# The last routing of a second expert stage placed in fewer tiles, and one exponential per routing

## The chip, the cores and the metric

The kernel runs on one core of a Trainium2 chip. Its five engines are TensorE (PE, with its weight loads shown as PEld), VectorE (DVE), ScalarE (ACT), GpSimd (POOL) and SyncE (SP); each works through its own queue of instructions in order, and they wait for each other by semaphores. The metric is the device time of one execution in microseconds; the number compared is the median of several executions.

## The reference

The program is a row of blocks on x of 16 x 256 = 4096 tokens with 128 features, all in float32: a mixture of experts, grouped-query attention, the same mixture of experts again, a block of eight "zones", a latent attention, and the zones again. Only the mixture of experts is touched. It is used twice with the same weights, each time as `x = x + 0.5 * ffn(layernorm(x))`:

```python
def _L0_ffn_ref(x, gate_w, experts_gate_up, experts_down, shared_gate_w, shared_up_w, shared_down_w, shared_expert_gate_w):
    logits = x_flat @ gate_w.T                       # 8 experts
    scores = softmax(logits)
    _, topk_ids = top_k(scores, 2)
    w = scores * one_hot(topk_ids).sum(axis=1)
    gu = einsum('nh,eih->nei', x_flat, experts_gate_up)   # 2 x 176
    h = silu(gu[..., :176]) * gu[..., 176:]
    out = einsum('neh,ne->nh', einsum('nei,ehi->neh', h, experts_down), w)
    shared = silu(x_flat @ shared_gate_w.T) * (x_flat @ shared_up_w.T) @ shared_down_w.T
    return out + sigmoid(x_flat @ shared_expert_gate_w.T) * shared
```

So each token has two of eight experts, weighted by their softmax scores, and a shared expert weighted by a sigmoid.

## The kernel before

The 4096 tokens are held in SBUF as eight blocks of 512 (`xs`), and routed in four pairs of blocks, 1024 tokens each (pairs 0 to 3). Each expert has a region of rows in DRAM (`moe_rows`). An expert stage has these parts:

*Routing of a pair* (`route_pieces`, fifteen pieces when it is coarse): four of statistics, a first guess and a refinement of the inverse root (VectorE), two that write the normalised tokens (`pair_xn`, half on ACT and half on VectorE), two that transpose them (TensorE, copies on VectorE and ACT), one for the logits of eight experts and, in a ninth column, of the sigmoid; then `choose` (VectorE: the two best experts), `count_before` (VectorE: prefix sums, and ACT: the exponentials), `place_pair` (three small matmuls, L579 to L585, turn the counts into a row for every token and choice; then sixteen indirect DMAs of POOL, L601, scatter the tokens to these rows) and `weights_of`. In `count_before` ACT computes exp of the logits less their maximum (L562, `moe_ex`) and, in a second instruction, exp of the negated ninth column (L565, `moe_ws`); the sigmoid follows on VectorE by L566 and L567. Exp and Silu are functions of different tables on ACT, and a change of table is an instruction of its own in the trace (ACT_TABLE_LOAD).

*Plans* (`plan_tiles`, three pieces by `table_pieces`): from the counts so far VectorE writes a table of tiles, each a run of 256 rows of one expert. Plans are made after two, three and four pairs. With two pairs 9 tiles are certain, with three 17, and the last plan has the rest of the 39. The last plan also makes SyncE read the eight counts (L658) and send eight stores of zeros (L665) behind the experts' last rows.

*Tiles* (`expert_tiles`): for each of the 39 tiles SyncE reads the table (L852), loads the expert's weights (L860, `moe_we`, six buffers) and the rows (L864, `moe_xg`, six buffers); TensorE transposes the rows (L881, copied to `moe_xT` by VectorE, L883), multiplies up (L893), ACT applies Silu (L895, L896), VectorE multiplies (L899, L902, into `moe_h` and `h`), TensorE multiplies down (L915, L920), ACT copies the result (L928) and sends it to DRAM (L929). Iteration k turns tile k, does up of tile k - 1 and down of tile k - 2, and then calls the pieces that `hooks[k]` names. Rows of tile 17 and later wait for all scatters of all four pairs; earlier ones only for those of the pairs that their plan knew.

After the tiles POOL gathers the results of each token (L956), VectorE adds them, and the remaining blocks of the shared expert (L803 to L832) are computed.

The first expert stage routes all four pairs before its tiles. The second one routes pairs 0, 1 and 2 beside attention (`beside_attention`), with the plans for two and three pairs; the routing of pair 3 and the last plan are hooks of its first tiles in `moe_second`. A tile scheduler puts instructions into the engines' queues by the order of the calls and by modelled times, so pieces of a hook are interleaved with tiles near it and not strictly behind one of them. PSUM tiles of kind `pb` have two buffers, shared by turns, transposes, logits and `place_pair`.

Of the kernel before, what the change touches and what calls it, by code (L numbers as in the profile page):

```python
# [12 lines left out]
F32 = mybir.dt.float32  # L13
I32 = mybir.dt.int32
U32 = mybir.dt.uint32
AF = mybir.ActivationFunctionType
ALU = mybir.AluOpType
# [3 lines left out]
P = 128  # L21
# [9 lines left out]
E0, I0, SI0, K0 = 8, 176, 352, 2  # L31
# [20 lines left out]
def macaron_kernel(ctx: ExitStack, tc: tile.TileContext, a: dict, out: bass.AP):  # L52
# [3 lines left out]
    nc = tc.nc  # L56
# [5 lines left out]
    small = ctx.enter_context(tc.tile_pool(name="small", bufs=3))  # L62
# [309 lines left out]
    NPT = 2 * NTT  # L372
# [46 lines left out]
    def begin_routing(S):  # L419
        shape = [P, NPAIR, K0, NPT]  # L420
        S["mine"] = routed.tile(shape + [E0], F32, name="moe_mine")
        S["at"] = routed.tile(shape, F32, name="moe_at")
        S["w"] = routed.tile(shape, F32, name="moe_w", bufs=2)
        S["index"] = routed.tile(shape, U32, name="moe_index", bufs=2)
        S["count"] = region_of

        S["row"] = region_of
        S["phases"] = []
# [87 lines left out]
    def choose_pieces(S, q):  # L516
        return [partial(choose, S, q), partial(count_before, S, q)]

    def choose(S, q):

        if q == 0:
            begin_routing(S)
        mine = S["mine"][:, q]
        shape = [P, NPT, E0]

        def wide(v):
            return v.unsqueeze(2).to_broadcast(shape)

        first = sooner.unsqueeze(1).to_broadcast(shape)
        lg = S["lg"][q]  # L530
        m = small.tile([P, NPT], F32, name="moe_m")
        nc.vector.tensor_reduce(m, lg[:, :, 0:E0], AX.X, ALU.max)
        less = small.tile(shape, F32, name="moe_less")
        nc.vector.tensor_tensor(less, lg[:, :, 0:E0], wide(m), ALU.subtract)
        key = small.tile(shape, F32, name="moe_key")
        nc.vector.scalar_tensor_tensor(key, less, 0.0, first, ALU.is_equal, ALU.mult)
        top = small.tile([P, NPT], F32, name="moe_top")
        nc.vector.tensor_reduce(top, key, AX.X, ALU.max)
        nc.vector.tensor_tensor(mine[:, 0], key, wide(top), ALU.is_equal)
        others = small.tile(shape, F32, name="moe_others")  # L540
        nc.vector.scalar_tensor_tensor(others, mine[:, 0], -3e38, less, ALU.mult, ALU.add)
        nc.vector.tensor_reduce(top, others, AX.X, ALU.max)
        nc.vector.tensor_tensor(key, others, wide(top), ALU.is_equal)
        nc.vector.tensor_tensor(key, key, first, ALU.mult)
        nc.vector.tensor_reduce(top, key, AX.X, ALU.max)
        nc.vector.tensor_tensor(mine[:, 1], key, wide(top), ALU.is_equal)
        S["less"][q] = less

    def count_before(S, q):

        mine = S["mine"][:, q]
        lg, less = S["lg"][q], S["less"][q]
        shape = [P, NPT, E0]
        s = sums[q % 2]
        now = slice(AHEAD, AHEAD + NPT)
        nc.vector.tensor_tensor(s[:, 0, now], mine[:, 0], mine[:, 1], ALU.add)
        for k in range(3):
            by = slice(AHEAD - 2**k, AHEAD - 2**k + NPT)
            nc.vector.tensor_tensor(s[:, k + 1, now], s[:, k, now], s[:, k, by], ALU.add)

        ex = small.tile(shape, F32, name="moe_ex")
        nc.scalar.activation(ex, less, AF.Exp)  # L562
        S["ex"][q] = ex
        ws = routed.tile([P, NPT], F32, name="moe_ws", bufs=NPAIR)
        nc.scalar.activation(ws, lg[:, :, E0], AF.Exp, scale=-1.0)  # L565
        nc.vector.tensor_scalar(ws, ws, 2.0, 2.0, ALU.mult, ALU.add)  # L566
        nc.vector.reciprocal(ws, ws)  # L567
        S["ws"][q] = ws

# [66 lines left out]
    def table_pieces(S, q):  # L636

        steps = []

        def piece(k):  # L640
            if k == 0:
                steps.append(plan_tiles(S, q))
            next(steps[0], None)

        return [partial(piece, k) for k in range(3)]
# [342 lines left out]
    def all_results(S):  # L988
        for t in range(2):
            fetch_results(S, t)  # L990
        for t in range(NBLK):
            pending[t] = add_results(S, t)

    def route_pieces(S, q, fine=False):
        return (
            pair_pieces(S, q, fine)
            + choose_pieces(S, q)
            + [partial(place_pair, S, q), partial(weights_of, S, q)]
        )
# [30 lines left out]
    def last_shared(S, t, end, after):  # L1030


        for k in range(t, end):
            pieces = shared_pieces(S, k)
            for f in pieces[:-1]:
                f()
            if k == t + 1:
                with tc.issue_after(added["up"].ins):
                    ready = after()
            pieces[-1]()  # L1040
        return ready
# [28 lines left out]
    def moe_second(S, after):  # L1070
        third = route_pieces(S, 3)
        hooks = {
            0: third[0:2],
            1: third[2:4],
            2: third[4:6],
            3: third[6:8],
            4: third[8:10],
            5: third[10:12],
            6: third[12:13],
            8: third[13:15],  # L1080
        }
        for k, f in enumerate(table_pieces(S, 4)):
            hooks[10 + k] = [f]
        for q in range(NPAIR):
            hooks[20 + 4 * q] = [partial(result_rows, S, q)]
        expert_tiles(S, hooks)
        all_results(S)
        return last_shared(S, 3, NBLK, lambda: after()())
# [714 lines left out]
    with in_pools(2, dict(pa=3)):  # L1803
        ready = moe_second(moes[1], partial(zones_pre, 0))
# [121 lines left out]
```

## Time and profile before

| | us |
|---|---|
| median of 4 runs | 1409.63 |
| lowest, highest | 1407.43, 1414.92 |
| the profiled execution | 1411.91 |
| its span | 1410.0 |

The stages by the profile's windows and lines: the first expert stage to about 200 us, attention to about 604 us, the tiles of the second expert stage from 604 to 721 us, its shared expert and results to about 767 us, then zones, latent attention and zones. Busy over the whole span: PE 1324.5 us (94%), DVE 953.0 (68%), ACT 668.1 (47%), POOL 448.8 (32%). The mean clock granted to TensorE is 0.983.

In the profile a line of a group or a timeline starts with its source line and engine; `out<-in` names the tiles written and read; a bracket at the end gives the time that the engine was idle before it and what ended that. SPq, ACTq and POOLq are the queues' own instructions, DMA issues among them.

### The profile page before, as it was taken

The numbers are of one execution on the slowest core, as the hardware profiler recorded it, in microseconds if no ns is written. First come the engines' busy times: TensorE is split into PE (matmuls) and PEld (weight loads), VectorE is DVE, ScalarE is ACT, GpSimd is POOL, SyncE is SP. The second block draws the span as 40 slices with busy tenths as digits, with TensorE's granted clock in tenths as the row PEclk, the third lists the DMA queues.
The fourth block names the chain that finished last, engine by engine and source line by source line (L and its number), as shares of the span: only waits on it lengthen the run. The fifth ranks groups of instructions, "written<-read, shape, count | busy, mean of one in ns | idle before, by whom it ended". The sixth has DMA issues, their size and how long they took to land.

```text
span 1410.0 us, 24848 instructions
## 1 busy us (share of the span) xinstructions
PE 1324.5 (94%) x7939; PEld 897.4 (64%) x7939; DVE 953.0 (68%) x3353; ACT 668.1 (47%) x1492; POOL 448.8 (32%) x515
## 2 busy tenths in 40 slices
PE   6898989999999999888999999999999999999998
PEld 4586754455555553466766878876555655688887
DVE  7755758788988874465757666665887888745341
ACT  4333421455555556343433334336777776634342
POOL 4770047420000404214027600014776765500000
PEclk9999999999999998999999999999999999999999
DMA  5297822100000100168834452520000000253532
GB/s 144 68 262 211 223 77 52 29 23 10 10 10 13 36 2 31 39 169 229 233 86 142 135 185 90 177 93 0 2 1 1 1 1 1 91 186 106 186 119 91
DMA packets 96497, 125.71 MB, mean 89 GB/s; under 512 B 12656, under 2 KB 68848, under 8 KB 96368
## 3 DMA queue, kind: packets, MB, share of 16 engines
q1 hardware_dynamic: 66960, 97.11, 22.5%
q0 software_dynamic: 8192, 16.79, 4.0%
q10 hardware_dynamic: 21216, 10.23, 2.4%
q8 instruction: 64, 1.05, 0.3%
q14 instruction: 65, 0.53, 0.1%
HBM read 98.40 MB, written 22.81 MB: 86 GB/s over the span
## 4 chain that ended last, share of the span: by engine, by line
PE 66%; DVE 19%; ACT 5%; DMA 3%; issue 3%; POOL 2%; SPq 1%; DVEq 0%; POOLq 0%; ACTq 0%
PE pb L1468 11%; PE pa L1454 10%; PE score L1197 6%; PE pb L1286 5%; PE exp L1209 4%; PE pa L893 3%; ACT ex L1640 3%; DVE nm L1633 3%; PE pa L803 3%; DMA moe_xg<-moe_rows 2%; PE score L1623 2%; PE pa L823 2%; PE pb L1582 2%; PE pa L915 1%; DVE pT L1670 1%
## 5 line engine op out<-in xcount | busy, mean ns | idle before, releaser
L1650 POOL TENSOR_SCALAR ex<-ex,rs 128x256 f32<-128x256 f32 x192 | 174.8, 928 | 69.2 <-DVE rs L1648 43.0
L956 POOL DMA_INDIRECT y<-moe_y,moe_index x128 | 124.1, 969 | 222.9 <-issue 194.7
L601 POOL DMA_INDIRECT moe_rows<-pair_xn,moe_slot x128 | 124.3, 971 | 201.0 <-DVE moe_slot L597 62.4
L1454 PE MATMUL pa<-xnT,zone_m 128*128 128x256 f32 x768 | 183.0, 381 | 2.0 <-DMA zone_m<-in_w_z_dram 1.1
L1462 ACT ACTIVATE zh<-pa 128x1024 f32<-128x1024 f32 x96 | 97.7, 1023 | 182.9 <-PE pa L1454 182.8
L1468 PE MATMUL pb<-zh,zone_m 128*128 128x256 f32 x768 | 176.8, 381 | 0.0
L1240 ACT ACTIVATE pT<-exp 128x512 f32<-128x512 f32 x224 | 124.2, 595 | 106.1 <-PE exp L1209 100.3
L1209 PE MATMUL exp<-qT,kT 32*128 32x512 f32 x480 | 168.6, 642 | 0.0
L1236 DVE TENSOR_REDUCE nm<-score 128x2 f32<-128x512 f32 x224 | 143.7, 683 | 33.1 <-PE exp L1209 32.2
L1197 PE MATMUL score<-kT,qT 32*128 32x256 f32 x960 | 163.7, 406 | 1.4 <-DVE nm L1236 1.2
L1468 PEld LDWEIGHTS pb<-zh,zone_m 128*128 128x128 f32 x768 | 144.7, 190 | 19.7 <-issue 0.3
L1454 PEld LDWEIGHTS pa<-xnT,zone_m 128*128 128x128 f32 x768 | 141.4, 190 | 23.3 <-DMA zone_m<-in_w_z_dram 2.4
L1197 PEld LDWEIGHTS score<-kT,qT 32*128 32x128 f32 x960 | 97.3, 184 | 80.9 <-DVE nm L1236 47.8
L1640 ACT ACTIVATE ex<-score,nm 128x256 f32<-128x256 f32 x256 | 117.5, 472 | 33.9 <-DVE nm L1634 22.4
L893 PE MATMUL pa<-moe_xT,moe_we 128*128 128x256 f32 (+1 forms) x468 | 118.3, 385 | 2.8 <-DVE moe_xT L883 2.1
L893 PEld LDWEIGHTS pa<-moe_xT,moe_we 128*128 128x128 f32 (+1 forms) x468 | 79.9, 186 | 15.5 <-DVE moe_xT L883 2.8
L895 ACT ACTIVATE moe_sg<-pa 128x256 f32<-128x256 f32 x78 | 29.9, 383 | 119.6 <-PE pa L893 119.6
L1633 DVE TENSOR_REDUCE nm<-score 128x4 f32<-128x1024 f32 x64 | 77.3, 1207 | 6.9 <-PE score L1623 6.9
L1668 PEld LDWEIGHTS turn<-ident,ex 128*128 128x128 f32 x512 | 57.5, 143 | 38.1 <-POOL ex L1650 21.1
L1623 PE MATMUL score<-kt,qa 64*128 64x256 f32 x512 | 78.0, 417 | 1.5 <-ACT ex L1640 1.5
L1668 PE MATMUL turn<-ident,ex 128*128 128x128 f32 x512 | 71.8, 281 | 5.3 <-ACT pT L1670 3.5
L1286 PE MATMUL pb<-pT,v 128*32 128x512 f32 x512 | 71.4, 626 | 2.8 <-ACT pT L811 1.5
(302 smaller groups left out, 2281.2 us busy)
## 6 DMA issues: line engine op xcount, KB each, us to landing
zone_m<-in_w_z_dram SPq DMA_DIRECT2D x96, 512.0 KB
moe_we<-in_w_ex_dram SPq DMA_DIRECT2D x78, 312.0 KB
moe_xg<-moe_rows SPq DMA_DIRECT2D x78, 128.0 KB
moe_y<-moe_yt ACTq DMA_DIRECT2D x78, 128.0 KB
x<-in_x_dram SPq DMA_DIRECT2D x8, 256.0 KB
moe_rows<-pair_xn,moe_slot POOLq DMA_INDIRECT x128
moe_rows<-zero_rows SPq DMA_DIRECT2D x16, 128.0 KB
y<-moe_y,moe_index POOLq DMA_INDIRECT x128
```

What stands on the lines that cost most here:

```text
L601: nc.gpsimd.indirect_dma_start(out=S["views"].pop()[:, :], out_offset=bass.IndirectOffsetOnAxis(ap=slot[:, k, i : i + 1], axis=0), in_=S[" ...
L893: nc.tensor.matmul(dst, q["w"][:, cols], q["xT"], start=True, stop=True)
L1197: nc.tensor.matmul(sc[:, j % 2, :], qa[rows, j, ts(b * NST + st, P)], kt[rows, ts(b, SEQ)], start=True, stop=True,)
L1209: nc.tensor.matmul(sc, kt[rows, ts(b * NST + s, P)], qa[rows, ts(half, 2), ts(b, SEQ)], start=True, stop=True,)
L1236: reduced["last"] = nc.vector.tensor_reduce(new["nm"][:, s, g1 + c, ts(half, 2)], scores[c], AX.X, ALU.max, negate=True)
L1240: nc.scalar.activation(old["pT", half][:, s, g0 + c, :], exps[c], AF.Exp)
L1286: nc.tensor.matmul(q["po"][ts(g, 32)], v[:, b * NST + s, ts(g, 32)], pT[:, s, g, :], start=(s == 0), stop=(s == NST - 1),)
L1454: nc.tensor.matmul(ps[:, f, :], mats[b * K1 + k][:, 0, ts(f, P)], xnT[:, ts(b, SEQ)], start=True, stop=True,)
L1468: nc.tensor.matmul(pz, mats[b * K1 + k][:, 1, ts(f, P)], h[:, f, :], start=(f == 0), stop=(f == NF1 - 1),)
L1640: nc.scalar.activation(ex[:, k, :], sc[:, k, :], AF.Exp, bias=nm[:, k : k + 1], scale=SCALE1, accum_out=rs[:, k : k + 1],)
L1650: nc.gpsimd.tensor_scalar(ex[:, k, :], ex[:, k, :], rs[:, k : k + 1], None, ALU.mult)
L1668: nc.tensor.transpose(pt[:, k, :], ex[:, k, ts(s, P)], ident)
```

## The change

Two things. In `choose` and `count_before` the negated ninth column is written by VectorE into a ninth column of the tile that already holds the logits less their maximum; one exponential of ACT over nine columns then serves the softmax and the sigmoid. This holds for all eight routings of the two stages. In `moe_second` the pieces of pair 3's routing are called at the hooks of tiles 0 to 4, four to a tile, instead of 0 to 8, two to a tile; `place_pair` stands at hook 3 instead of 6, and the three pieces of the last plan at hooks 8 to 10 instead of 10 to 12.

```diff
@@ choose
-        less = small.tile(shape, F32, name="moe_less")
+
+        both = small.tile([P, NPT, E0 + 1], F32, name="moe_less")
+        less = both[:, :, 0:E0]
         nc.vector.tensor_tensor(less, lg[:, :, 0:E0], wide(m), ALU.subtract)
...
-        S["less"][q] = less
+        nc.vector.tensor_scalar(
+            both[:, :, E0 : E0 + 1], lg[:, :, E0 : E0 + 1], -1.0, None, ALU.mult
+        )
+        S["less"][q] = both
@@ count_before
-        ex = small.tile(shape, F32, name="moe_ex")
-        nc.scalar.activation(ex, less, AF.Exp)
-        S["ex"][q] = ex
+        ex = small.tile([P, NPT, E0 + 1], F32, name="moe_ex")
+        nc.scalar.activation(ex, S["less"][q], AF.Exp)
+        S["ex"][q] = ex[:, :, 0:E0]
         ws = routed.tile([P, NPT], F32, name="moe_ws", bufs=NPAIR)
-        nc.scalar.activation(ws, lg[:, :, E0], AF.Exp, scale=-1.0)
-        nc.vector.tensor_scalar(ws, ws, 2.0, 2.0, ALU.mult, ALU.add)
+        nc.vector.tensor_scalar(ws, ex[:, :, E0], 2.0, 2.0, ALU.mult, ALU.add)
         nc.vector.reciprocal(ws, ws)
@@ moe_second
         hooks = {
-            0: third[0:2],
-            1: third[2:4],
-            2: third[4:6],
-            3: third[6:8],
-            4: third[8:10],
-            5: third[10:12],
-            6: third[12:13],
-            8: third[13:15],
+            0: third[0:4],
+            1: third[4:8],
+            2: third[8:12],
+            3: third[12:13],
+            4: third[13:15],
         }
         for k, f in enumerate(table_pieces(S, 4)):
-            hooks[10 + k] = [f]
+            hooks[8 + k] = [f]
```

More of the change, by code (lines that the diff above doesn't have):

```diff
@@ L546, in choose @@
         nc.vector.tensor_tensor(mine[:, 1], key, wide(top), ALU.is_equal)
-        S["less"][q] = less
+        nc.vector.tensor_scalar(
+            both[:, :, E0 : E0 + 1], lg[:, :, E0 : E0 + 1], -1.0, None, ALU.mult
+        )
+        S["less"][q] = both
     def count_before(S, q):
         mine = S["mine"][:, q]
-        lg, less = S["lg"][q], S["less"][q]
-        shape = [P, NPT, E0]
         s = sums[q % 2]
```

## The prediction, made before the changed kernel was run

> **What bounds the kernel now.** The program is one row of stages, and only two are touched in a way that can move the end: the routing beside the first tiles of the second expert stage (604 to 721 us) and, by one small edit, each of the eight routings. I first cut that stage into three windows (busy us, and count, of PE, PEld, DVE, ACT, POOL; then clock, DMA share, GB/s).
>
> ```profile
> 604.00:634.00 30.00, 26.36 (x165) 20.97 (x164) 22.25 (x86) 16.26 (x34) 1.92 (x2) 1.00 0.69 189
> 634.00:671.00 37.00, 31.28 (x184) 23.54 (x183) 20.80 (x74) 13.57 (x36) 15.36 (x16) 1.00 0.80 224
> 671.00:721.00 50.00, 49.35 (x303) 39.65 (x303) 34.31 (x115) 21.11 (x56) 0.00 (x0) 1.00 0.74 204
> ```
>
> From 671 us on TensorE works 49.35 of 50 us: nothing is to be had there. The 67 us before hold 57.64 us of matmuls, so some 9.4 us of idle time is the most that better timing of routing and plan could give. The list of waits of TensorE between 600 and 730 us (total, times, longest) says what ends that idle time:
>
> ```profile
> PE pb L881 <- DMA moe_xg<-moe_rows: 5.0, 6, 1.8
> PE pa L893 <- DVE moe_xT L883: 2.1, 3, 1.3
> PE pa L915 <- DVE h L902: 1.8, 5, 0.6
> ```
>
> The gathered rows of a tile come late, six times; the rest is VectorE. Next the timeline of TensorE, SyncE's queue and POOL (start, us, what, [idle before, and its releaser]):
>
> ```profile
> 649.49 0.44 PE L881 MATMUL pb<-ident,moe_xg 128*128 128x128 f32 x2 [1.39 <-DMA moe_xg<-moe_rows]
> 659.77 0.44 PE L881 MATMUL pb<-ident,moe_xg 128*128 128x128 f32 x2 [1.81 <-DMA moe_xg<-moe_rows]
> 663.04 0.44 PE L881 MATMUL pb<-ident,moe_xg 128*128 128x128 f32 x2 [0.91 <-DMA moe_xg<-moe_rows]
> 671.13 1.46 PE L893 MATMUL pa<-moe_xT,moe_we 128*128 128x256 f32 x6
> 673.66 1.46 PE L893 MATMUL pa<-moe_xT,moe_we 128*128 128x256 f32 x6
> ```
> ```profile
> 638.66 0.34 SPq L860 DMA_DIRECT2D moe_we<-in_w_ex_dram  x1
> 641.92 4.37 SPq L665 DMA_DIRECT2D moe_rows<-zero_rows  x8
> 646.47 0.40 SPq L864 DMA_DIRECT2D moe_xg<-moe_rows  x1
> 654.13 0.35 SPq L860 DMA_DIRECT2D moe_we<-in_w_ex_dram  x1
> 657.64 0.37 SPq L864 DMA_DIRECT2D moe_xg<-moe_rows  x1
> ```
> ```profile
> 634.60 0.96 POOL L601 DMA_INDIRECT moe_rows<-pair_xn,moe_slot  x1 [28.30 <-DVE moe_pick L625]
> 653.56 0.96 POOL L601 DMA_INDIRECT moe_rows<-pair_xn,moe_slot  x1 [0.30 <-issue]
> ```
>
> I count tiles by the matmul groups of L893, six records a tile: 9 groups start before 634.8 us, 6 more before 653.5 and 5 more before 671.1, so those that start at 626.55, 645.68, 653.57 and 671.13 us are tiles 7, 13, 15 and 20. An undisturbed tile takes 673.66 - 671.13 = 2.53 us. Two things are late. First, SyncE's queue: the weights of tile 14 go out at 638.66, then come the last plan's counts and eight zero stores (641.92 for 4.37 us), and only at 646.47 the rows of tile 14: 7.8 us without a fetch, and TensorE waits 1.39 us for them at 649.49. Second, the sixteen scatters of pair 3 on POOL: 634.60 to 653.56, that is 18.96 / 15 = 1.264 us each; the last lands 3.75 us after its start by the chain of waits, and tile 17, the first that needs it, has its rows asked for only at 657.64, 3.16 us behind its weights (654.13 + 0.35). TensorE waits 1.81 and 0.91 us. From tile 15 to tile 20 it takes 671.13 - 653.57 = 17.56 us instead of 5 x 2.53 = 12.65.
>
> **The change part by part.** *One exp for a routing.* Removed, eight times: one ACT exponential of 128x8 (0.16 us from PSUM, 0.22 from SBUF, rows of L565). Added, eight times: one VectorE multiply of 128x8; the row of L566, same form, takes 0.16 us. The remaining exp is 72 wide instead of 64: 0.256 us, at most 72/64 of that, +0.03. Beside attention (250 to 450 us TensorE is busy 197.08 of 200) I cost this at nothing; without that cover it is 3 x 0.16 = 0.5 us. In the first stage the multiply stands ahead of the first scatter, and the new order of instructions also puts one 128x512 multiply (L812, 0.68 us) ahead of the prefix sums and one normalise (0.26) and one statistic (0.2) behind them: +0.1 + 0.6 - 0.3 - 0.2 = +0.2 us to the first scatter at 24.12. POOL then works through 64 scatters without a gap, so the first tiles and the last plan inherit +0.2. The other pairs have room: slots of pairs 2 and 3 are ready at 48.7 and 65.8 us, POOL reaches them at 24.12 + 32 x 1.266 = 64.6 and 84.9. Bounds: -0.5 (the removed exps all count, 8 x 0.16 less the multiplies) to +0.7 (the L812 in full).
>
> *Table loads.* In the order of instructions four table loads go, because a routing's two exps no longer straddle a Silu. The rows:
>
> ```profile
> 621.36 1.28 ACT L562 ACT_TABLE_LOAD   x1 [0.43 <-ACT moe_yt L928]
> 623.68 1.28 ACT L895 ACT_TABLE_LOAD   x1
> 626.15 1.28 ACT L565 ACT_TABLE_LOAD   x1
> 627.64 1.28 ACT L895 ACT_TABLE_LOAD   x1
> ```
>
> One pair goes here (626.15, 627.64), one at 576.36 and 582.03. At 582.03 the load stands before a Silu whose input is ready near 582.6, which then starts at 583.33; a place matmul at 583.98 waited 0.41 us for it. I take -0.4 there, bounds 0 and -1.3 (the whole load). The pair in the tile stage is inside the next term.
>
> [...] Here each load is 1283 ns and the activation behind it starts 10 to 20 ns later, so no drain is seen. [...]
>
> *Routing in half as many tiles.* The same instructions, earlier, and in the new order nearly all between tiles 0 and 5: statistics before tile 0, transposes and logits behind tile 2, the choice behind tile 4's turn, the place matmuls behind tile 4. VectorE is in order, so I follow it from the trace's rows. 1.2 us of statistics (609.19 to 610.41) and one turn copy (0.34) and one gate product (1.0) no longer stand ahead of the normalise: 615.80 becomes 613.2. Transposes end with ACT's four normalises (1.65) at 615.4, logits (1.9) at 617.2. Then the first delay: the exp waits behind the table load and the mask until 618.7, the second load ends at 620.0, tile 3's gates at 620.8. VectorE puts 13 operations of the choice and 4 sums, 0.26 us apart, ahead of tile 3's gate product, which thus ends at 623.5; TensorE waits some 1.2 us for the sums, then 0.8 for tile 5's copy behind the eight operations of the placing. Tile 7 starts near 630.6 instead of 626.55. Of these 4.0 us, 0.6 is place work that stood behind tile 7 before; the rest is lost, early. If VectorE costs nothing, TensorE's own work (7 ups of 1.30, 8 turns of 0.37, 6 downs of 0.87, 3.9 of routing) puts tile 7 at 626.9: that is one bound. The other is 633.5, if each handover from ACT to VectorE costs one operation more.
>
> *Plan two tiles sooner.* On SyncE the counts and zero stores now stand two fetches earlier, before the rows of tile 12. Their start hangs on the buffer of tile 6, down of which ends about 632.8; before it was tile 8's, 637.9, with the weights out at 638.66. So weights 12 go out at 633.5, 5.1 us sooner, and the same 7.8 us hole moves with them: rows 12 at 641.3, rows 13 at 644.8 and tile 13 at 644.8 + 3.64 = 648.4 (before: rows 15 at 649.93, tile 15 at 653.57). Behind SyncE's hole are all later rows and weights; nothing else waits on it. Tile 15 follows at 648.4 + 2 x 2.53 = 653.5: level with before.
>
> *The scatters.* Slots are ready near 625.0, so POOL runs 625.3 to 645.2 and the last lands at 625.3 + 18.96 + 3.75 = 648.0. Rows of tile 17 are asked for at 644.8 + 4 x 2.37 = 654.3 (2.37 is SyncE's step, 649.93 to 652.30): 6 us of room. The wait for scatters goes, and tiles 15 to 20 take 12.65: -4.9 us. POOL had been idle 28.30 us, so nothing is displaced on it.
>
> [...]
>
> **Sum.** +0.2 - 0.4 + 0 (tile 15 level) - 4.9 = -5.1 us. The profiled span is 1410.0 (the run 1411.91, so 1.9 lies around it); the median of the four runs is 1409.63, and I take the difference from that: 1404.5. Later stages follow the second stage's end one for one: its result gathers start only when the tiles are done.
>
> **Rivals.** *More of the idle time goes.* If the head costs what TensorE's own work says (tile 7 at 626.9), SyncE's hole starts 3.7 us sooner and tile 20 with it: -8.8, 1400.8. For: POOL's scatters are then done at 645, and rows keep 2.37 us a step, faster than TensorE. Against: VectorE's 22.25 of 30 us in this window, with more in fewer tiles. *It gives nothing.* If SyncE's hole costs more two tiles earlier, because the fetches have had less time to run ahead, the saved 4.9 come back as waits for rows 12 to 16: 1409.4. For: DMA is at 0.80 in that window already. Against: weights 12 wait on a buffer, as weights 14 did, so the lead is the same. *Slower: ACT and VectorE lock step.* The sigmoid weight now needs the joint exp, and VectorE's queue holds that reader in the middle of the choice; the exp stands on ACT behind four normalises, two copies and a table load. If it comes late, the gate products of tiles 3 and 4 stand behind it and TensorE has nothing. It decides once tile 7 starts later than 630.6 + 5.1 = 635.7; at 645, two missed rounds of some 7 us (ACT 3.5 us of normalise and copies, VectorE 3.5 of choice), it gives 1409.6 + 9 = 1419. Against: the exp is ready 2 us before its reader by my count.
>
> **How the numbers follow.** Forecast, between -1 and -9: 0.50, own range 1400 to 1408.5. More goes: 0.27. Nothing: 0.12. Slower: 0.11. A measurement of this kernel can tell about 0.5%, 7.0 us, from no change. Faster by that needs 1402.6 or less: three in four of the second case and two in five of the first, 0.40; slower (1416.7 or more) nearly all of the last, 0.10; the rest, 0.50, is within. The range leaves out the slower case and the far end of the better one: 1398 to 1412.
>
> **What would show it.** The profile after should have 47 table loads on ACT instead of 51; first scatter of pair 3 in the second stage near 625; tile 7 near 630.6; zero stores near 636.8 with TensorE still waiting 1 to 3 us for rows 12 and 13; no wait for rows 17 and 18; the chain without the sixteen scatters of that stage. Wrong would be a tile 13 far from 648.4, or rows still waiting for POOL.

## The result, and the profile after

| | before | changed |
|---|---|---|
| median, us | 1412.21 (73 runs) | 1415.19 (48 runs) |
| lowest, highest | 1406.1, 1416.89 | 1404.7, 1423.49 |
| profiled execution, and its span | 1411.91, 1410.0 | 1408.67, 1406.9 |

The ratio of the runs is 1.0024 (95% interval 1.0015 to 1.0034): slower by 0.24%, 3.4 us (the medians differ by 3.0), where 5.1 us less was forecast; 1415.19 lies outside the range of 1398 to 1412. The profiled execution of the changed kernel is one of its quicker ones (only four of the 48 took less), so its stages have to be read against more executions than one. (In the section on the change, `place_pair` is the piece at hook 4, before at hook 8; 3 and 6 are those of `count_before`.)

First the list of waits of TensorE between 600 and 730 us after (total, times, longest). The six waits for rows have become one:

```profile
PE pb L883 <- DMA moe_xg<-moe_rows: 2.6, 1, 2.6
```

Next the timelines after, POOL, SyncE's queue and TensorE, as shown of before:

```profile
624.65 0.96 POOL L603 DMA_INDIRECT moe_rows<-pair_xn,moe_slot  x1 [21.16 <-DVE moe_pick L627]
```
```profile
633.62 0.35 SPq L862 DMA_DIRECT2D moe_we<-in_w_ex_dram  x1
637.13 4.42 SPq L667 DMA_DIRECT2D moe_rows<-zero_rows  x8
641.73 0.40 SPq L866 DMA_DIRECT2D moe_xg<-moe_rows  x1
645.18 0.37 SPq L866 DMA_DIRECT2D moe_xg<-moe_rows  x1
...
654.91 0.37 SPq L866 DMA_DIRECT2D moe_xg<-moe_rows  x1
...
662.37 0.37 SPq L866 DMA_DIRECT2D moe_xg<-moe_rows  x1
```
```profile
612.89 2.00 PE L498 MATMUL pb<-w_rt,moe_xnT 128*128 128x9 f32 x16 [0.35 <-DVE moe_xnT L478]
...
617.40 2.77 PE L895 MATMUL pa<-moe_xT,moe_we 128*128 128x256 f32 x6
...
620.82 1.87 PE L895 MATMUL pa<-moe_xT,moe_we 128*128 128x256 f32 x6
...
630.14 1.46 PE L895 MATMUL pa<-moe_xT,moe_we 128*128 128x256 f32 x6
...
645.95 0.69 PE L883 MATMUL pb<-ident,moe_xg 128*128 128x128 f32 x2 [2.57 <-DMA moe_xg<-moe_rows]
647.21 2.90 PE L895 MATMUL pa<-moe_xT,moe_we 128*128 128x256 f32 x6 [0.56 <-issue]
...
652.04 1.19 PE L895 MATMUL pa<-moe_xT,moe_we 128*128 128x256 f32 x4
```
```profile
670.24 1.46 PE L895 MATMUL pa<-moe_xT,moe_we 128*128 128x256 f32 x6
```

POOL starts the sixteen scatters 10 us sooner, and the transfers stand where the prediction put them: zero stores at 637.13 (636.8 forecast), rows of tile 12 at 641.73 (641.3), of tile 13 at 645.18 (644.8), of tile 17 at 654.91 (654.3), with no wait for a scatter. But tile 13 starts at 652.04, not 648.4, and two of the groups of six up matmuls (L893 before, L895 now), those of tiles 3 and 12, take 2.77 and 2.90 us, where an undisturbed group takes 1.46. The windows say why (us, busy time and count of TensorE, granted clock, DMA share, GB/s):

```profile
603.00:611.30 8.30, 6.90 (x37) 1.00 0.68 177
611.30:614.70 3.40, 3.05 (x27) 0.99 0.90 229
614.70:621.50 6.80, 6.80 (x22) 0.50 0.43 129
621.50:645.30 23.80, 20.92 (x132) 1.00 0.84 230
645.30:652.20 6.90, 5.68 (x19) 0.51 0.72 209
```

In two stretches of this stage the granted clock is 0.50. The profile of before has 1.00 throughout the stage (a second profile of the kernel before, h0 below, has one such stretch). The first stretch follows the transposes and logits of pair 3, which now stand in a row; the second follows the 2.57 us in which TensorE waits for the rows of tile 12.

### The profile page after: what moved, and what is told of

It is laid out like the page before. It is cut to its first block, busy times and chain, and to the rows that moved or that the text cites. A ratio compares the mean times of both kernels' runs of the same rounds, so it can differ in the third digit from the quotient of the medians.

```text
span 1406.9 us, 24867 instructions
## 1 busy us (share of the span) xinstructions
PE 1324.6 (94%) x7939; PEld 903.2 (64%) x7939; DVE 952.4 (68%) x3361; ACT 662.7 (47%) x1480; POOL 447.4 (32%) x515
## 4 chain that ended last, share of the span: by engine, by line
PE 63%; DVE 17%; issue 7%; ACT 6%; DMA 3%; POOL 2%; SPq 1%; POOLq 0%; DVEq 0%; ACTq 0%
PE pb L1467 12%; PE pa L1453 10%; PE pa L895 5%; PE score L1196 4%; ACT ex L1639 4%; PE exp L1208 3%; PE pb L1285 3%; PE pa L805 3%; DVE nm L1632 2%; PE pa L917 2%; PE pa L825 2%; PE pa L922 2%; PE score L1622 2%; PE pb L1581 1%; PE pb L883 1%
## 5 line engine op out<-in xcount | busy, mean ns | idle before, releaser
L1196 PEld LDWEIGHTS score<-kT,qT 32*128 32x128 f32 x960 | 97.1, 183 | 80.0 <-DVE nm L1235 47.8
L1639 ACT ACTIVATE ex<-score,nm 128x256 f32<-128x256 f32 x256 | 117.7, 473 | 32.9 <-DVE nm L1633 21.5
L895 PE MATMUL pa<-moe_xT,moe_we 128*128 128x256 f32 (+1 forms) x468 | 122.6, 397 | 3.6 <-DVE moe_xT L885 2.3
L895 PEld LDWEIGHTS pa<-moe_xT,moe_we 128*128 128x128 f32 (+1 forms) x468 | 83.2, 193 | 17.5 <-DVE moe_xT L885 2.9
```

Of the source, the lines that this page charges most:

```text
L895: nc.tensor.matmul(dst, q["w"][:, cols], q["xT"], start=True, stop=True)
L1196: nc.tensor.matmul(sc[:, j % 2, :], qa[rows, j, ts(b * NST + st, P)], kt[rows, ts(b, SEQ)], start=True, stop=True,)
L1639: nc.scalar.activation(ex[:, k, :], sc[:, k, :], AF.Exp, bias=nm[:, k : k + 1], scale=SCALE1, accum_out=rs[:, k : k + 1],)
```

## The experiments

Every kernel was timed against the kernel before on the same chip. The runs fell on two kinds of chip: on chips 11 and 3 the kernel before took 1411 to 1412 us, on chips 15, 12 and 7 it took 1611 to 1614, and the profiles from there show ACT and VectorE stopped for long whiles (last section). Ratios are read within a kind. Medians are in us, intervals are 95%. The theories A, B and C are told in the first expectation, D in that of g2.

| run | chip | median, before beside it | ratio (interval) |
|---|---|---|---|
| e1 joint exponential alone | 15 | 1612.46, 1611.46 | 1.0015 (0.9986 to 1.0045) |
| e2 hooks alone | 15 | 1611.62, 1611.46 | 1.0014 (0.9982 to 1.0046) |
| e4 changed, plan late | 15 | 1624.26, 1611.46 | 1.0073 (1.0042 to 1.0103) |
| e5 changed, eight buffers | 15 | 1612.18, 1611.46 | 1.0010 (0.9976 to 1.0044) |
| f1 joint exponential alone | 12 | 1615.34, 1611.47 | 1.0020 (0.9994 to 1.0045) |
| f2 hooks alone | 12 | 1615.49, 1611.47 | 1.0043 (1.0018 to 1.0067) |
| f3 changed | 12 | 1622.79, 1611.47 | 1.0067 (1.0046 to 1.0088) |
| f5 changed, eight buffers | 12 | 1609.98, 1611.47 | 0.9988 (0.9967 to 1.0009) |
| g5 changed, block 3 in the head | 7 | 1620.71, 1613.90 | 1.0044 (1.0026 to 1.0062) |
| g2 changed, stores spread | 7 | 1621.35, 1613.90 | 1.0052 (1.0031 to 1.0073) |
| g3 before, eight buffers | 7 | 1597.86, 1613.90 | 0.9906 (0.9888 to 0.9923) |
| g6 all together | 7 | 1605.72, 1613.90 | 0.9936 (0.9913 to 0.9959) |
| h0 before | 11 | 1413.96 (one), 1411.78 | |
| h1 joint in the second stage only | 11 | 1411.66, 1411.78 | 1.0009 (0.9990 to 1.0027) |
| h2 block 3 whole | 11 | 1423.05, 1411.78 | 1.0090 (1.0068 to 1.0112) |
| h3 before, eight buffers | 11 | 1416.68, 1411.78 | 1.0036 (1.0020 to 1.0053) |
| k1 joint exponential alone | 3 | 1413.86, 1411.67 | 1.0011 (0.9991 to 1.0032) |
| k2 hooks alone | 3 | 1412.86, 1411.67 | 1.0010 (0.9996 to 1.0023) |

**Each part alone.** The edit of e1, f1 and k1 is the change with the old hooks; that of e2, f2 and k2 is the new hooks with two exponentials (the five lines of the hooks are written as one here):

```diff
+        0: third[0:4], 1: third[4:8], 2: third[8:12], 3: third[12:13], 4: third[13:15],
...
-            hooks[10 + k] = [f]
+            hooks[8 + k] = [f]
```

> The joint exponential alone; the routing of pair 3 and the last plan stay at the tiles they had before. Theory A (the loss is made in the head of the second expert stage by the denser routing, which leaves TensorE thin or idle long enough for its granted clock to fall to 0.50): ratio to before 0.998 to 1.000, since the joint exponential saves a table load of 1.28 us here and there. Theory B (the loss comes from the new order of instructions that the one exponential brings in the first expert stage, where the profile of the changed kernel shows low clock near 24, 34 and 116 us that the profile of before does not): ratio 1.002 to 1.004. Theory C (SyncE's hole of 7.8 us costs more two tiles earlier): 0.998 to 1.000.

> The hooks of the second stage alone; each routing keeps its two exponentials. Theory A: ratio 1.002 to 1.005, the profile with low clock between 610 and 660 us in most executions. Theory B: 0.996 to 0.998, the 4 to 5 us of the scatters' wait. Theory C: 1.001 to 1.004, with a wait for rows 12 of 2 us or more and full clock.

> The joint exponential alone, on a chip without the long stops of the first four runs. Theory A (clock lost in the head of the second expert stage by the denser routing): ratio 0.998 to 1.000. Theory B (new order of instructions in the first expert stage): 1.002 to 1.004. Theory C (SyncE's hole two tiles earlier): 0.998 to 1.000.

> The hooks alone. Theory A: ratio 1.002 to 1.005, with clock of 0.50 between 610 and 660 us. Theory B: 0.996 to 0.998. Theory C: 1.001 to 1.004, with a wait for rows 12 of 2 us or more and full clock around it.

> The changed kernel once more, for a second profile beside the others on the same chip. All theories: ratio 1.0015 to 1.0034 as measured. Theory A: clock of 0.50 between 610 and 660 us again, in one or two stretches of 3.4 or 6.8 us. Theory B: low clock between 20 and 130 us, more than the 10.2 us of the profile of before.

> The joint exponential alone, where engines do not stop for POOL. If the loss is made in the first stage: ratio 1.001 to 1.003, the place matmul of pair 0 near 22.8 us and low clock near 24 us. If it is made in the second stage's head: 0.998 to 1.000.

> The hooks alone, where engines do not stop for POOL. If the loss is made in the second stage's head: ratio 1.001 to 1.003, low clock near 11.7 and 42.4 us after tile 0's up, tile 20 at 66 to 67 us after it (65.4 in the kernel before). If it is made in the first stage: 0.997 to 1.000, tile 20 below 65 us.

(The f runs were meant for a chip without the stops, and fell on one with them.) All six ratios lie above 1, though only f2's interval leaves 1 out; on chip 3 the two parts give 1.0011 and 1.0010, which add up to about the 1.0024 of the whole. f3 repeats the sign of the result on another chip, larger than forecast for it (1.0067, where 1.0034 was the most). So neither theory A nor theory B has it alone: both halves of the change seem to cost something, and the 5.1 us of gain is nowhere. On chip 3 each ratio fits the case that puts the loss into its own half, but the marks named for these cases do not tell them apart: k1 has low clock at 23.3 us, as the kernel before has at 22.2 in h0, and k2 has the first low stretch 11.1 us after tile 0, none near 42.4, and yet tile 20 at 68.0 us, later than the 66 to 67 expected.

**The clock in the dense head.** The changed kernel (f3) and the one with the late plan (e4) issue the same instructions on TensorE up to tile 7. Their timelines, f3 first, show the logits and the up groups of tiles 3 and 4:

```profile
762.61 2.06 PE L498 MATMUL pb<-w_rt,moe_xnT 128*128 128x9 f32 x16 [0.35 <-DVE moe_xnT L478]
...
767.17 2.77 PE L895 MATMUL pa<-moe_xT,moe_we 128*128 128x256 f32 x6
...
770.59 1.81 PE L895 MATMUL pa<-moe_xT,moe_we 128*128 128x256 f32 x6
```
```profile
764.88 1.95 PE L498 MATMUL pb<-w_rt,moe_xnT 128*128 128x9 f32 x16 [0.35 <-DVE moe_xnT L478]
...
768.17 1.46 PE L895 MATMUL pa<-moe_xT,moe_we 128*128 128x256 f32 x6
...
769.98 1.56 PE L895 MATMUL pa<-moe_xT,moe_we 128*128 128x256 f32 x6
```

From the logits to the up of tile 4 it takes 770.59 - 762.61 = 7.98 us in the one and 769.98 - 764.88 = 5.10 in the other. The window behind the logits, f3 and then e4 (columns as above):

```profile
764.40:771.20 6.80, 6.80 (x22) 0.50 0.41 129
```
```profile
766.70:773.50 6.80, 6.52 (x40) 1.00 0.67 199
```

The same stretch holds 22 matmuls at clock 0.50 and 40 at 1.00. The clock records of the trace change only at multiples of 3.413 us from one another within an execution; the profiles of before and of the changed kernel have 21 such changes each, and each stretch at 0.50 in them lasts 3.4, 6.8 or 10.2 us, but for the last, which the end of the trace cuts off. For all executions with the dense head and six buffers, this gives the place of that grid against tile 0's up (time modulo 3.413 us), how long the clock was at 0.50 after the logits, and the time from tile 0 to tile 7:

```
             grid, us   clock 0.50 for   tile 0 to tile 7
e4             0.16         0                24.6
e2             0.22         0                24.4
k2             0.84         6.8              27.2
g2             0.94         6.8              27.2
f3             1.38         6.8              27.2
h1             1.41         6.8              27.1
changed        1.44         6.8              27.2
f2             2.52         3.4              25.7
```

So nearly the same instructions pay 0, 1.2 or 2.6 us here, and what they pay goes by where the grid happens to stand; none of the profiles with the old routing (both of before, e1, f1, k1, g3, h3) has low clock at this place. Why the clock falls is not shown by these runs. In the changed kernel's execution TensorE was busy 3.05 of the 3.40 us ahead of the drop (611.30 to 614.70 us), with transposes and 9-column logits, and only 2.49 of 3.30 us in the stretch ahead of that (608.00 to 611.30), which no drop followed; so busy time in the profile did not keep the clock up here. Which property of these matmuls counts was not tested.

**SyncE's hole.** Edits: the plan at hooks 10 to 12 as before (e4); eight buffers instead of six (e5, f5; g3 and h3 in the kernel before); the stores one or two between fetches (g2).

```diff
-            hooks[8 + k] = [f]
+            hooks[10 + k] = [f]
```
```diff
-            w = pool.tile([P, W0], F32, name="moe_we", bufs=6)
+            w = pool.tile([P, W0], F32, name="moe_we", bufs=8)
...
-            xg = pool.tile([P, half, D], F32, name="moe_xg", bufs=6)
+            xg = pool.tile([P, half, D], F32, name="moe_xg", bufs=8)
```
```diff
-            for r in rows:
-                nc.sync.dma_start(S["views"].pop()[ds(r, SLOTS), :] ...)
+            S["zeros"] = [partial(zero, r) for r in rows]
...
+        for k in range(E0):
+            hooks.setdefault(9 + k, []).append(lambda k=k: S["zeros"][k]())
```

> The changed kernel, but the three pieces of the last plan stay at hooks 10 to 12; the routing is at hooks 0 to 4 and the exponential is joint. Theory A: the dense routing and its low clock near 614 us stay, the wait for rows 14 comes when tiles 9 to 13 have built a lead, so ratio 1.000 to 1.002. Theory B: as the changed kernel, 1.002 to 1.003. Theory C: 0.996 to 0.998, as the hole is back where it was before and the scatters' wait is gone.

> The changed kernel with eight buffers instead of six for the weights and the rows of a tile, so that SyncE runs up to two tiles further ahead and its hole of 7.8 us lies under TensorE's work. Theory A: the wait of 2.6 us for rows 12 goes and with it the low clock near 645 us, but not that near 614 us: ratio 0.997 to 1.000. Theory B: 1.001 to 1.003, since the first part of the first stage is unchanged. Theory C: the whole loss goes, ratio 0.995 to 0.997.

> The changed kernel with eight buffers instead of six for weights and rows of a tile. Theory A: no wait of 2.6 us for rows 12 and full clock near 645 us; ratio 0.997 to 1.000. Theory B: 1.001 to 1.003. Theory C: 0.995 to 0.997.

> The changed kernel; in the second stage the eight zero stores go out one or two between two fetches instead of all eight at once. Theory D (SyncE's hole two tiles earlier makes TensorE wait 2.6 us for rows 12, and this idle time brings the second stretch of low clock, 42 us after tile 0's up): no wait for rows above 1 us and no low clock there where engines do not stop for other reasons; 3 to 6 us below the changed kernel, ratio to before 0.999 to 1.002. Rival (the queue's total work counts, not its lump): waits of about 0.5 us at several tiles instead of one, ratio as the changed kernel, 1.002 to 1.007.

> The kernel before with eight buffers instead of six for weights and rows of a tile. If SyncE's hole costs it about 1.4 us a stage and buffers hide it, ratio 0.998 to 0.999; the wait for the scatters (1.8 and 0.9 us) stays. If eight buffers helped the changed kernel only because its hole is where the tiles have no lead, 1.000.

> The kernel before with eight buffers once more, on another chip where one is given, since 0.991 was more than was expected of it: 0.989 to 0.993 if it holds, 0.998 to 0.999 if only the fetch holes of the two stages go.

The late plan did not help (1.0073; the changed kernel itself ran on another of these chips, with 1.0067), and spreading the stores did not either (1.0052): theory C, that the hole costs more for standing two tiles earlier, is not carried by these. On these chips a stop of the engines covers tiles 8 to 10, so the wait for rows 12 could not be seen by itself. Eight buffers took the changed kernel to 1.0010 and 0.9988, and the kernel before to 0.9906; but on chip 11, without the stops, the same kernel is at 1.0036. That is a lesson on chips with stops, not on the hole, and why eight buffers cost there is open.

**Useful work in the thin stretch.** In g5 the up products of the shared expert of block 3 stand beside the dense routing; its down product and the addition to x are left out there, and so they are in g6. In h2 the block is whole; what it adds is the down product alone (its expectation also names a third up product, which g5 had). g6 is the hooks of g5 with two exponentials and eight buffers. The edit of h2:

```diff
+        extra = shared_pieces(S, 3)
...
-            2: third[8:12],
-            3: third[12:13],
-            4: third[13:15],
+            2: extra[0:1] + third[8:12],
+            3: extra[1:3] + third[12:13],
+            4: extra[3:4] + third[13:15],
...
-        return last_shared(S, 3, NBLK, lambda: after()())
+        return last_shared(S, 4, NBLK, lambda: after()())
```

> The changed kernel, with the shared expert of block 3 (useful work that otherwise runs behind the tiles) put beside the dense routing at hooks 2 to 4, so that full-size matmuls stand between the transposes and the logits of pair 3. Theory A (the thin stretch of transposes and 9-column logits makes the clock fall to 0.50 some 11.7 us after tile 0's up, for 3.4 to 6.8 us): no low clock between 8 and 22 us after that up, tiles 0 to 8 take at most 6 us more than the 29.7 us of the changed kernel although 6.1 us of matmuls were added, and the total is 3 to 6 us below the changed kernel's: ratio to before 1.000 where the changed kernel stands at 1.004. Rival (VectorE's dense queue is the cost, not the clock): the added products of block 3 lengthen it, tiles 0 to 8 take 8 us more or above, and the ratio stays at that of the changed kernel, 1.002 to 1.007.

> A version to beat both: two exponentials as before, the early dense hooks, block 3's shared expert beside them, eight buffers. If the three costs named so far are the whole loss (first stage's order by the joint exponential, the thin stretch, the rows of tile 12), what is left is the scatters' 4.9 us and what block 3 hides: ratio 0.992 to 0.996. If the dense head itself is the cost: 1.000 to 1.004.

> As the run with block 3's shared expert beside the dense routing, but now whole: the third product of two up and the down product, which the first attempt left out. Theory A: no low clock between 8 and 22 us after tile 0's up; tiles 0 to 5 take 23 to 25 us (22.0 in the changed kernel) with 6 to 8 us more matmuls among them; ratio 0.002 to 0.003 below the changed kernel's. Rival (VectorE's queue): 27 us or more, ratio not below.

g6's 0.9936 fits its first case, but beside g3's 0.9906 on the same chip it is the eight buffers that gain there, and the rest of g6 gives some of it back. In the head the clock stays up, in g5 and in h2 (1.00 from 613 to 626 us). The grid stands at 1.20 us in h2, among the places where the unfilled head lost 6.8 us of clock, and at 0.50 in g5, between places with a loss and without; it is one execution of each. The windows of h2 (head, then the stretch between the last tile and the first zone) and the same last stretch of before:

```profile
613.00:626.00 13.00, 13.00 (x80) 1.00 0.60 168
724.40:775.80 51.40, 39.17 (x179) 0.91 0.23 64
```
```profile
719.70:767.60 47.90, 44.92 (x212) 1.00 0.32 95
```

Tiles 0 to 5 take 25.4 us in h2: just beyond theory A's 23 to 25 and below the rival's 27. Yet the kernel is 0.9% slower, which neither expected. Behind the tiles, block 3's work had filled TensorE while POOL gathers results; without it TensorE is busy 39.17 of 51.40 us instead of 44.92 of 47.90, waits 5.6 us once for a gate product, and the clock falls to 0.91 on the mean. In this execution, then, the work had been taken from a place that needed it.

**The first stage.** Its routing with two exponentials, the joint one in the second stage only, and the kernel before once more for its profile (the start of h1's edit):

```diff
+        joint = S["pool"]() is routed
+        if joint:
             both = small.tile([P, NPT, E0 + 1], F32, name="moe_less")
```

> The kernel before itself, for a profile under the conditions of these runs, where ACT and VectorE stop for up to 40 us while POOL issues indirect DMAs. First stage: tiles 0 to 38 take about 116.5 us (as with the hooks alone) if the joint exponential is what costs there, 121 us if not; second stage: 125 to 126 us, as with the joint exponential alone.

> The changed kernel, but the first stage keeps its two exponentials and with them its order of instructions; the joint one is used in the second stage only. If the joint exponential costs 3 to 4 us in the first stage (place matmul 1.1 us later, TensorE idle 2.5 us before it, low clock after it): tiles 0 to 38 of that stage 116 to 117 us instead of 120 to 122, ratio to before about 0.002 lower than the changed kernel's, 1.003 to 1.005. If the first stage does not matter: 1.006 to 1.007.

Both fell on a chip without the stops, so the stage times forecast for them do not apply. h1's 1.0009 is below its 1.003 to 1.005: it lies between the kernel before and the changed one, and beside the hooks alone (1.0010), which speaks for a cost of the joint exponential in the first stage of up to 0.0015; the intervals allow none. By the starts in the traces on chips without stops, in us:

```
                 first    last up,   attention's last   tile 0   tile 0    tile 0
                 scatter  stage 1    scores to tile 0   to 8     to 20     to 38
before            24.1     180.3         76.5            25.8     65.4     112.8
h0 before         23.7     181.7         75.5            25.8     64.9     112.6
k1 joint alone    24.7     180.8         73.7            24.2     63.0     110.4
k2 hooks alone    23.8     180.1         75.4            29.7     68.0     115.7
h1                23.7     180.4         73.8            29.7     66.9     114.6
changed           25.2     181.7         74.0            29.7     67.3     115.2
```

The place matmul of pair 0 shows how the joint exponential delays the first scatter, before and then after:

```profile
21.68 0.41 PE L579 MATMUL pb<-sums,every 128*128 128x64 f32 x2 [1.55 <-DVE sums L559]
```
```profile
22.80 0.41 PE L581 MATMUL pb<-sums,every 128*128 128x64 f32 x2 [2.50 <-DVE sums L562]
```

The first scatter is 0.6 to 1.5 us later with it, but the end of the stage's tiles moves less than the two profiles of before differ among themselves: in the three profiles that have it (k1, h2, changed) the stage's 39 tiles take 107.9 to 108.0 us instead of 103.6 to 106.0, but start 2 to 4 us sooner. What the joint exponential costs on the median is thus not found in a place on these chips: k1's profiled execution, with its short stages, took 1404.38 us, the least of its twelve, whose median is 1413.86. On the chips with stops it does show: with six buffers the last up of the first stage starts at 231.5 to 236.9 us in the six profiles that have the joint exponential there (e1, f1, e4, f3, g2, g5), and at 229.5 and 228.5 us in the two that have not (e2, f2).

## Why the prediction was wrong, point by point

*First stage, +0.2.* The first scatter came 1.1 us later (24.12 to 25.2), above the bound of 0.7 named: TensorE waited 2.50 us for the sums instead of 1.55. By the ends of the tiles that is +1.4 in the profiled execution; h0 against before shows that 1.4 is also what chance does. (The lower bound of -0.5 does not come out of its own working: eight times 0.16 removed and eight times 0.16 added make nothing.) What this half costs in the median is below.

*Table loads, -0.4.* The loads went as counted, four of 51. The stretch from attention's last scores to tile 0 takes 73.7 to 74.0 us in the three profiles with the joint exponential in the second stage and 75.4 to 76.5 in the three without: about -2. A part of that is chance of the clock, 0 to 10.2 us of half clock in this stretch; at the same 3.4 us, h1 against h0 and k2, it is -1.6 to -1.7. So the sign was right and the size, with its bound of -1.3, too small on these chips; on those with stops the stretch is 103 to 106 us with the joint exponential and without. That it is the two loads that make the difference was argued from their count, not shown alone.

*The head: tile 7 near 630.6.* It came at 630.14, but that is luck: the stage began at 602.98, and the forecast counted from before's 605.72. From tile 0 it is 27.2 us instead of 24.9. In the executions without low clock it is 24.6 and 24.4. So the estimate of VectorE's queue was not too low; what was left out is 2.6 us of half clock.

*Plan and fetches: rows 13 at 644.8 + 3.64 = tile 13 at 648.4, tile 15 level with before.* This is the step that failed, the sum's term "0 (tile 15 level)". The fetches came to 0.6 us as forecast, but only because the earlier start and the late head cancel: from tile 0, weights of tile 12 go out at 30.6 us instead of 27.8, and rows of tile 13 at 42.2 instead of 39.1. The 3.64 us from rows 13 to tile 13 were taken from a stretch at full clock; they became 652.04 - 645.18 = 6.86 us, since TensorE, after its 2.57 us of idling for rows 12, worked the next 6.8 us at 0.50. From tile 0 to tile 15 it took 54.3 us, not the 47.8 forecast and 47.9 before: 3.1 of the 6.5 us come from the late fetch, 3.2 from tile 13. The second stretch of half clock is not needed for the loss, though. In k2 the clock is 1.00 behind the head and tile 13 comes 3.9 us after its rows are asked for; but these, too, are asked for late, at 42.6 us, tile 15 stands at 52.3, and then TensorE waits for later rows until tile 20 at 68.0. Its list of waits, between 600 and 730 us:

```profile
PE pb L881 <- DMA moe_xg<-moe_rows: 4.9, 7, 1.9
```

*Scatters: -4.9.* Right in the changed kernel: tiles 15 to 20 take 670.24 - 657.26 = 12.98 us instead of 17.56 (13.0 in h1, but 15.7 in k2). POOL's step is (643.60 - 624.65) / 15 = 1.263 us (1.264 before), beside a VectorE that is busy 16.27 of the 23.8 us from 621.5 to 645.3. While the scatters start (the sixteen within 18.95 us, before 18.96), VectorE is busy 13.92 us now (624.65 to 643.60) and was busy 12.55 before (634.60 to 653.56), and the step did not grow. But the gain is worth less than a row of its own. Rows of tile 20 are asked for 59.4 us after tile 0 in both kernels (662.37 - 602.98, and 665.10 - 605.72 before): behind its hole SyncE's queue steps by some 2.4 us a tile and is where it was, with the scatters or without. The hole moved two tiles ahead started only 30.6 us after tile 0 (before: 32.9), since it hangs on the buffer of tile 6, which the slow head gave back late. And the wait for scatters had been a cushion before: in h0 TensorE waits 2.85 us for rows 14 and then has 6.8 us of half clock as well, and tile 20 still stands at 64.9 us, because the waits at tiles 17 and 18 shrink by what was lost. In the changed kernel nothing behind tile 15 gives it back.

So tiles 0 to 20 were to take 47.8 + 12.65 = 60.4 us, 5.0 less than before, and take 67.3, 1.9 more, in the profile of the changed kernel, with two stretches of half clock in it, which the sum did not have at all: it took TensorE's clock as constant because the profile of before showed 1.00 in this stage.

The median is another matter. The changed kernel's profiled execution is 3.2 us shorter than that of before, and most of this comes from the stages behind, which the change does not touch: from the first product of the zones to the end they take 639.6 us instead of 642.4, with 7.1 us of half clock instead of 14.1. So two profiles cannot be subtracted to explain 3.4 us. The executions of the tables have their mean granted clock on record: 0.9817 in 50 of the changed kernel, 0.9828 in the 46 of before on chips 11 and 3, 0.9811 in the twelve of k2, 0.9813 in those of h1, 0.9842 in those of k1. A straight line of time against clock, with one slope for all kernels timed without the stops, gives 0.93 us for 0.001 (standard error 0.10). By it about 1.0 us of the changed kernel's loss is lost clock, and 1.4 and 1.6 us for k2 and h1 against the runs of before beside them, which is all that these two are slower. At the same clock the kernels stand from before at +2.8 us (changed), +2.3 (k1), +0.1 (k2) and -0.5 (h1), with standard errors of 0.6 for the changed kernel and 0.9 for the others. The two that have the joint exponential in the first stage are slower beyond their clock, the two that have not are level. So the larger part of the 3.4 us seems to be a cost of the joint exponential in the first stage, where the sum had +0.2, and the smaller part lost clock, which the profiles show behind tile 0. This is worked out after the fact from runs on several chips, not shown by a run made for it, and where in the program these 2 to 3 us are paid stays open.

*The rivals.* "It gives nothing" was nearest, by its mechanism in part (SyncE's hole eats the saved wait) and by its difference of -0.2 us from before. "Slower: lock step" had the right sign and the wrong cause: its point of decision, tile 7 later than 635.7, was not reached.

No version tried beats the kernel before on a chip without stops; h1, the changed kernel with the first stage as it was, equals it within its interval.

## What to carry to other kernels

When a change packs thin TensorE work (transposes, few-column matmuls) together or makes one longer wait out of several short ones, price it at full clock and at half clock, and give each case its chance: in this head the loss (0, 1.2 or 2.6 us) went by where a grid of 3.413 us happened to lie, and the profile of before is one draw. Before booking a wait as a gain, look at what stands behind it in the same queue, and whether other losses are paid from it now. A profiled execution at the edge of its kernel's times cannot say what the median pays; compare the times at the same granted clock as well, over all executions on record.

## What the runs showed of the hardware that was not expected

The kernel before takes 1411 us on some chips and 1611 on others. On the latter engines stop with a releaser that the trace doesn't know. In the timeline of VectorE and POOL of f3:

```profile
298.47 0.35 DVE L834 SCALAR_TENSOR_TENSOR x<-pa,moe_ws,x 128x128 f32<-128x128 f32 x1 [33.45 <-remote]
```
```profile
242.08 0.98 POOL L958 DMA_INDIRECT y<-moe_y,moe_index  x1 [110.60 <-issue]
243.36 0.96 POOL L958 DMA_INDIRECT y<-moe_y,moe_index  x1 [0.30 <-issue]
...
291.42 0.95 POOL L958 DMA_INDIRECT y<-moe_y,moe_index  x1 [0.30 <-issue]
```

VectorE stands for 33.45 us while POOL issues gathers. There are some 264 us of such stops on VectorE and ACT in that execution, and each one ends during a run of POOL's indirect DMAs or within 8 us of its end; the profiles from chips without stops have none, and POOL's own instructions take the same 0.96 us on both. Moving the sixteen scatters of pair 3 only moved the stop (tile 12 in e1, tiles 8 to 10 in f3). The cause was not looked for. It also means that a ratio from one kind of chip need not hold on the other: eight buffers gave 0.9906 and 1.0036.
